# A two-layer graph network on one core: second-layer scores and weights moved behind other products, and adds of the output unit given to GpSimd

## The chip, the core and the metric

The kernel runs on one core of a Trainium2 chip. Its time is the device time of one execution in microseconds; the median of three runs is 2927.16 us (2926.97 to 2927.3). Engines are named TensorE (PE in the profile; its weight loads PEld), VectorE (DVE), ScalarE (ACT), GpSimd (POOL) and SyncE (SP, which issues the DMAs). Each engine works through its own instructions in the order in which the program gives them, and waits where an instruction needs what another engine has not finished.

## What is computed

64 graphs of 256 nodes with 512 features share one adjacency matrix; all is float32. Layer 0 is multi-head attention over neighbours, layer 1 a graph attention with one head, both with a layer norm and a ReLU ahead and a residual add behind:

```python
h = jnp.maximum(_layernorm(x, axis=-1), 0.0)
q, k, v = (h @ Wq + bq, h @ Wk + bk, h @ Wv + bv)        # 8 heads of 64
attn = softmax(q k^T / 8 + (1 - adj) * -1e9)
x = x + (attn v) @ Wo + bo
h = jnp.maximum(_layernorm(x, axis=-1), 0.0)
h = einsum('bnc,cf->bnf', h, W); s1, s2 = h @ a1, h @ a2
e = leaky_relu(s1[:, :, None] + s2[:, None, :], 0.2) * mask
x = x + elu(softmax(e, axis=2) @ h + beta * h)
```

## The kernel before, in words

**Pairs and products.** Graphs are worked on in pairs (32 of them, p = 0 to 31; graphs 2p and 2p+1). A product of a pair with a weight matrix is cut into 2 x 2 blocks (graphs by halves of the features), and seven block products take the place of eight (the Winograd form of Strassen's scheme). A `Unit` (L270) makes them: `p(i)` issues product i on TensorE. Products 1, 4, 5, 6 and 7 start a new PSUM bank (1 into `a`, 4 into `d`, 5 into `b`, 6 and 7 into `k`); product 2 adds into `a`, product 3 into `b`. With product 1 ScalarE copies `a` to `u2` (L283), with 6 VectorE adds `k` to `u2` (L285), with 7 it makes `u3` (L288). `products` (L640) calls `put11` after product 2, `put2` after 5 and `put12` after 3; these take the four blocks out of PSUM. Since product 3 adds into the bank of product 5, `put2` must have read that bank before. There are two QK units (queries and keys, L348), a V unit (L393), an O unit (L474) and a W unit (L579) for each pair. A QK product is 4 + 4 matmuls in the trace, the others 8.

**Layer 0.** `scores(b)` (L413): queries by keys (L422) into eight banks, the exponential on ScalarE (L426), the mask product and a pair sum on GpSimd (L427, L429). `values(b)` (L444): the weighted values (L440) and the row sums (L449) on TensorE; on VectorE a reciprocal (L451), the sums added to a running total `acc` for the range check (L452), the product (L454), and the reciprocal added to `acc` too (L455). `residual` (L468) loads the residual input y by DMA and adds the bias on GpSimd (L472); `o_blocks` (L458) forms two block sums on GpSimd (L464). The O unit's results are added to y: one VectorE operation for block (0,0) (L482), two for each of the other three (L486 and L487, or L492 and L493).

**Layer 1.** Statistics of y (L248), scales (VectorE L255, GpSimd L258 to L260, ScalarE L266), normalised h on ScalarE (L509). `node_sums` (L512) multiplies h by the projected attention vectors and sums, two operations for each tile of 128 nodes (L515). `gat_scores` (L518): two TensorE transposes spread the sums (the tile `pe`, L171), then on VectorE L525 twice and L527. `gat_exp` (L529): exponentials on ScalarE. `gat_divide` (L534): the weights, with beta on their diagonal (L539 twice). `gat_t` (L542): TensorE transposes them (the tile `at`, L548), ScalarE copies them (L549). `z_graph` (L551): h by weights (the tile `pz`, L561). Then the W unit and the ELU (L586 to L602), whose result goes out by DMA.

**Order.** It is written out by hand, the same for all engines: `start` (L719), `first` (L778), then for each pair `first_half` (L807) and `second_half` (L842), and `last` (L887) and `end` (L934) for the last pairs. The first half of pair p holds the V unit of pair p with the second layer's scores and weights of pair p-2 among its products (`v_chain`, L873), z and the W unit of pair p-2, and the O unit of pair p-1. The second half holds the rest of that O unit, the values of graph 2p, the scores of 2p+1, the QK units of pair p+1 with norms, node sums and `gat_scores` of graph 2p-1 among their products, and the values and scores that follow. At the start the weights' block sums (L120 to L123) and the projections of the attention vectors (L227) are put among the first pairs' work, and `in_range` (L701) checks at the end that no sum left the safe range; a general path runs only if one did.

Of the kernel before, what the change touches and what calls it, by code (L numbers as in the profile page):

```python
# [23 lines left out]
def kernel(ctx: ExitStack, tc: tile.TileContext, x, adj, wq, bq, wk, bk, wv, bv, wo, bo, w, a, beta, out):  # L24
# [65 lines left out]
    acc = const.tile([P, N], F32, name="acc")  # L90
    nc.gpsimd.memset(acc, 0.0)
# [9 lines left out]
    def weight(name, src, permuted=False):  # L101

        raw = const.tile([P, 3, 2, N], F32, name=f"{name}_b")
        b12 = blk("set", f"{name}_b12")
        tt = const.tile([P, 4, 2, N], F32, name=f"{name}_t")

        def fetch(*which):
            for j in which:
                dst, r, f = ((raw[:, 0], 0, 0), (raw[:, 1], 1, 0), (b12, 0, 1), (raw[:, 2], 1, 1))[j]
                if permuted:  # L110
                    for i in range(4):
                        nc.sync.dma_start(dst[i * HH:(i + 1) * HH], wo_rows(src)[r, i, :, :, f * N:(f + 1) * N])
                else:
                    nc.sync.dma_start(dst, rows_in_order(src)[r, :, :, f * N:(f + 1) * N])

        b11, b21, b22 = (raw[:, i] for i in range(3))
        t1, t2, t3, t4 = (tt[:, i] for i in range(4))

        def sums():
            nc.vector.tensor_tensor(t1, b12, b11, ALU.subtract)  # L120
            nc.vector.tensor_tensor(t2, b22, t1, ALU.subtract)
            nc.vector.tensor_tensor(t3, b12, b22, ALU.subtract)
            nc.vector.tensor_tensor(t4, b21, t2, ALU.subtract)  # L123

        return {1: b11, 2: b21, 3: b22, 4: t4, 5: t1, 6: t2, 7: t3}, b12, fetch, sums
# [47 lines left out]
    def project_b():  # L173


        WO, b12, fetch, sums = weight("wo", wo, True)
        fetch(*range(4))
        nc.sync.dma_start(bo2, bo.partition_broadcast(P))
        bvc = sb([P, DC], "bvc", "bvc", 1)
        with nc.allow_non_contiguous_dma(reason="a bias, once"):  # L180
            bv_v = bv.rearrange("(q i s d) -> i d q s", q=2, i=4, s=2, d=HH)
            for i in range(4):
                for q in range(2):
                    nc.sync.dma_start(bvc[i * HH:(i + 1) * HH, 2 * q:2 * q + 2], bv_v[i, :, q, :])
        cbs = []

        def part(n):
            if n == 0:
                sums()
            elif n == 1:  # L190
                for c in range(DC):
                    if c % 2 == 0:
                        cbs.append(sb([P, 2, P], "rec", f"bvb_{c}"))
                    nc.vector.tensor_scalar(cbs[-1][:, c % 2, :], ones, bvc[:, c:c + 1], None, ALU.mult)
            else:
                ps = bank("pbo")
                for c in range(DC):
                    for f in range(2):
                        b = ((WO[1], b12), (WO[2], WO[3]))[c // 2][f]
                        nc.tensor.matmul(ps[:, f * N:(f + 1) * N], cbs[c // 2][:, c % 2, :], b[:, c % 2, :],  # L200
                                         start=(c == 0 and f == 0), stop=(c == DC - 1), skip_group_check=True)
                nc.vector.scalar_tensor_tensor(bo2, bo2, -1.0, ps, op0=ALU.add, op1=ALU.add)

        return WO, part

    def project_a():
# [3 lines left out]
        sums()  # L210
# [28 lines left out]
        return part  # L239
# [62 lines left out]
    def combine_2(s):  # L302
        s[6] = blk(s["tag"], f"s2_{s['name']}")
        nc.vector.tensor_tensor(s[6], s[5], s[1], ALU.subtract)

    def combine_4(s):
        s[3] = blk(s["tag"], f"s4_{s['name']}")
        nc.vector.tensor_tensor(s[3], s[2], s[6], ALU.subtract)
# [135 lines left out]
    def values(b):  # L444
        for q in range(2):
# [6 lines left out]
            nc.vector.tensor_tensor(acc, sums[:, :N], acc, ALU.add)  # L452
            OT[b, q] = blk("set", f"oT_{b}_{q}")
            nc.vector.tensor_tensor(OT[b, q], two(ps), rec.unsqueeze(1).to_broadcast([P, 2, N]), ALU.mult)  # L454
            nc.vector.tensor_tensor(acc, acc, rec, ALU.add)  # L455
# [18 lines left out]
    class UnitO(Unit):  # L474

        def __init__(self, p):
            self.pair = p
            super().__init__(f"o_{p}", nodes_mm(A["o", p], WO))

        def put11(self):  # L480
            y = Y[2 * self.pair, 0]
            nc.vector.tensor_tensor(y, two(self.a), y, ALU.add)  # L482

        def put(self, gi, fh, ps, u):
            y = Y[2 * self.pair + gi, fh]
            nc.vector.tensor_tensor(two(ps), two(ps), u, ALU.add)  # L486
            nc.vector.tensor_tensor(y, two(ps), y, ALU.add)  # L487

        def put2(self):

            y = Y[2 * self.pair + 1, 1]
            nc.vector.tensor_tensor(two(self.k), two(self.b), self.u3, ALU.add)  # L492
            nc.vector.tensor_tensor(y, two(self.k), y, ALU.add)  # L493
            self.put(1, 0, self.d, self.u3)

        def put12(self):
            self.put(0, 1, self.b, self.u2)
# [81 lines left out]
    class UnitW(Unit):  # L579

        def __init__(self, p, tag=None):

            self.pair, self.o, self.tag = p, {}, tag
            super().__init__(f"w_{p}", nodes_mm(A.pop(("z", p)), WW))

        def elu(self, gi, fh, src, o=None, step=None):  # L586
# [7 lines left out]
            if step is not False:  # L594
                o, m, y = self.o[gi, fh]
                nc.vector.scalar_tensor_tensor(o, src, 0.0, y, op0=ALU.max, op1=ALU.add)  # L596
# [14 lines left out]
        def put2_sums(self):  # L611
            self.c = blk(self.tag or "c", f"o_{2 * self.pair + 1}_1")
            nc.vector.tensor_tensor(self.c, two(self.b), self.u3, ALU.add)
            nc.vector.tensor_tensor(two(self.d), two(self.d), self.u3, ALU.add)

        def put2_elu(self, step=None):

            self.elu(1, 1, self.c, self.c, step)
            self.elu(1, 0, two(self.d), None, step)

        def put12(self):
            nc.vector.tensor_tensor(two(self.b), two(self.b), self.u2, ALU.add)
            self.elu(0, 1, two(self.b))
# [65 lines left out]

    def residuals(p, which, tag="y"):  # L690
        for gi, fh in which:
# [9 lines left out]
    def in_range():  # L701
        bad = sb([P, 3], "bad", "bad", 1)
        for j, (src, op, bound) in enumerate(((acc, ALU.is_le, SAFE), (gsums, ALU.is_le, SAFE),
# [15 lines left out]
    def start():  # L719
# [24 lines left out]
        wo_blocks, shift = project_b()  # L744
# [19 lines left out]
        prods = project_a()  # L764
        products(uv, 4, 6)
        shift(1)
# [4 lines left out]
        shift(2)  # L771
# [4 lines left out]
        return wo_blocks, prods  # L776

    def first(prods):  # L778
# [4 lines left out]
        products(ua, 1, 4, 6, 2, 7, 5)  # L783
# [3 lines left out]
        products(ub, 4, 6, 7, 5, 2, 3)  # L787
        prods(3)
        prods(4)
# [5 lines left out]
        products(uv, 1, 4, 6, 2, 7, 5)  # L795
# [46 lines left out]
    def second_half(p, uo):  # L842
# [19 lines left out]
        ub.p(4)  # L862
        gat_scores(g1 - 2)
        gat_exp(g1 - 2)
        ub.p(6)
        y_sums(p - 1, 0, 0)
        products(ub, 7, 5)
# [5 lines left out]
    def v_chain(p):  # L873
# [7 lines left out]
        products(uv, 6, 2)  # L881
        gat_t(2 * p - 3)
        gat_t(2 * p - 4)
        products(uv, 7, 5)
        return uv

    def last():  # L887
# [6 lines left out]
        residuals(p - 1, ((0, 0), (1, 1), (1, 0), (0, 1)), "qk")  # L894
# [4 lines left out]
        uo = UnitO(p - 1)  # L899
# [4 lines left out]
        uw = UnitW(p - 2, "set")  # L904
# [4 lines left out]
        products(uw, 4)  # L909
        values(g1)  # L910
        y_normal(p - 1, 1)
        y_normal(p - 1, 0)
        residuals(p, ((0, 0), (1, 1)), "qk")
        o_blocks(p)
        residuals(p, ((1, 0), (0, 1)), "qk")
        products(uw, 6)
        y_sums(p - 1, 1, 0, 1)
        products(uw, 2, 7)
        uw.finish(0, 0, nc.gpsimd)
        gat_scores(g1 - 2)  # L920
        gat_exp(g1 - 2)
        uw.p(5)
        uw.put2_sums()
        uo = UnitO(p)
        uo.p(1)
        y_sums(p - 1, 0, 0)
        uw.put2_elu(False)
        uw.p(3)
        combine_24(A["o", p])
        y_sums(p - 1, 0, 1)  # L930
        uo.p(4)
        return uw, uo

    def end(uw, uo):  # L934
        p = NP - 1
        g0, g1 = 2 * p, 2 * p + 1
        products(uo, 2)
        uo.p(6)
        gat_scores(g0 - 2)
        gat_exp(g0 - 2)  # L940
        uw.put2_elu(True)
        uw.put12()
        uw.finish(1, 1, nc.gpsimd)
        uw.finish(1, 0, nc.gpsimd)
        uw.finish(0, 1, nc.gpsimd)
        products(uo, 7)
        divide(p - 1)
        products(uo, 5)
        y_stats(g1, NT, 0, g1, 1)
        y_stats(g1, NT, 0, g1, 0)  # L950
        rstd, mr = scales(f"y{g1}", 2)
        gat_t(g1 - 2)
        gat_t(g0 - 2)
        normal(g1, rstd, minus(mr, f"y{g1}"), "v")
        y_stats(g0, NT, 0, g0, 0)
        products(uo, 3)
        y_stats(g0, NT, 0, g0, 1)
        rstd, mr = scales(f"y{g0}", 2)
        z_graph(p - 1, 0)
        z_graph(p - 1, 1)  # L960
        normal(g0, rstd, minus(mr, f"y{g0}"), "v")
        y_sums(p, 1, 0, 1)
        gat_scores(g1)
        z_31(p - 1)
        gat_exp(g1)
        z = A["z", p - 1]
        combine_2(z)
        uw = UnitW(p - 1, "pt")
        products(uw, 1, 4)
        y_sums(p, 0, 0, 1)  # L970
        products(uw, 6)
        gat_divide(ATT[g1], gsums[:, NT * g1:NT * g1 + NT], g1)
        uw.p(2)
        gat_scores(g0)
        gat_exp(g0)
        uw.p(7)
        gat_t(g1)
        uw.put11()
        uw.p(5)
        uw.put2_sums()  # L980
        combine_4(z)
        uw.finish(0, 0, nc.gpsimd)
        z_graph(p, 1)
        gat_divide(ATT[g0], gsums[:, NT * g0:NT * g0 + NT], g0)
        uw.p(3)
        gat_t(g0)
        uw.put2_elu()
        uw.put12()
        uw.finish(1, 1, nc.gpsimd)
        uw.finish(1, 0, nc.gpsimd)  # L990
        uw.finish(0, 1, nc.gpsimd)
        bad = in_range()
# [4 lines left out]
        combine_24(A["z", p])  # L997
        uw = UnitW(p, "pt")
        uw.p(1)
        uw.p(4)  # L1000
        uw.p(6)
        uw.p(7)
# [12 lines left out]
    with tc.manual_schedule(engines={ENG.PE, ENG.DVE, ENG.Activation, ENG.Pool}):  # L1015
        WW = {}
        WO, prods = start()
        second_half(1, first(prods))
# [166 lines left out]
```

## Time and profile before

| | |
|---|---|
| median of 3 runs | 2927.16 us |
| profiled execution: its time, its span | 2926.01 us, 2924.1 us |
| granted TensorE clock, mean | 0.998 |
| instructions | 46443 |
| VectorE: L515, 256 times | 253.7 us, mean 1.04 us |
| VectorE: L451, 128 times | 224.3 us, mean 1.75 us |
| VectorE: L452 and L455, 128 times each | 46.4 and 92.5 us |
| GpSimd: L427, 512 times | 710.8 us, mean 1.39 us |
| DMA | 110 MB, 38 GB/s over the span |

The span is from the first to the last instruction of the profiled execution. In lists of instructions each line has the start in us from the beginning of the span, the duration, engine, line of the program, operation, the tiles (written <- read), the shapes and the count; a bracket at the end gives the idle time of the engine before it and what ended that.

### The profile page before, as it was taken

To read this page: it belongs to the slowest core of one execution; us is meant where nothing else is said; L and a number is where in the kernel's file an instruction comes from. 1 tells how busy PE (TensorE), PEld (TensorE's weight loads), DVE (VectorE), ACT (ScalarE), POOL (GpSimd) and SP (SyncE) were. 2 spreads that over 40 slices of the span, in tenths; PEclk is the share of its full clock that TensorE was granted. 3 is DMA by queue.
4 is the path that set the end of the run, shared out by engine and by line. 5 is a ranking of instruction groups with operands and counts; after the bars stand their busy time and mean duration, and the time that the engine had idled before them with its cause. 6 is when DMAs were issued, how large, how long until landed. Compare 5 with 4: busy or idle time off the path is not lost.

```text
span 2924.1 us, 46443 instructions
## 1 busy us (share of the span) xinstructions
PE 2815.4 (96%) x18110; PEld 2344.7 (80%) x18110; DVE 2158.2 (74%) x3779; ACT 1035.7 (35%) x2116; POOL 1525.4 (52%) x1464
## 2 busy tenths in 40 slices
PE   9999999999999999999999999999999999999998
PEld 7887788787888878888778887788787888878876
DVE  7677877777777677776787777877777777678776
ACT  3233334333333333333343333334333333333323
POOL 4645545455454554545554545545455454555572
PEclk9999999999999999999999999999999999999999
DMA  5010011100111100111001110011100111100101
GB/s 148 5 44 17 28 44 44 44 23 29 37 44 44 33 26 30 44 44 44 15 30 44 44 44 20 26 44 44 44 27 26 37 44 44 33 26 30 37 30 44
DMA packets 96479, 110.00 MB, mean 38 GB/s; under 512 B 8576, under 2 KB 79488, under 8 KB 96256
## 3 DMA queue, kind: packets, MB, share of 16 engines
q1 hardware_dynamic: 96256, 106.99, 11.7%
q8 instruction: 145, 2.38, 0.3%
q14 instruction: 78, 0.64, 0.1%
HBM read 73.41 MB, written 33.55 MB: 37 GB/s over the span
## 4 chain that ended last, share of the span: by engine, by line


## 5 line engine op out<-in xcount | busy, mean ns | idle before, releaser
L427 POOL TENSOR_TENSOR pt<-pt,maskT 128x512 f32<-128x512 f32 x512 | 710.8, 1388 | 799.9 <-ACT pt L426 799.9
L429 POOL TENSOR_TENSOR pp<-pt 128x256 f32<-128x256 f32 x512 | 429.1, 838 | 40.1
L426 ACT ACTIVATE pt<-sc 128x512 f32<-128x512 f32 x512 | 257.7, 624 | 411.2 <-PE sc L422 411.2
L451 DVE RECIPROCAL rec<-sm 128x256 f32<-128x256 f32 x128 | 224.3, 1753 | 46.5 <-PE sm L449 46.5
L515 DVE SCALAR_TENSOR_TENSOR pr<-h,war 128x512 f32<-128x512 f32 x256 | 253.7, 1035 | 0.0
L440 PE MATMUL av<-pt,v 128*32 128x256 f32 x4096 | 246.0, 381 | 0.7 <-DVE v L410 0.7
L422 PE MATMUL sc<-qk 64*128 64x256 f32 x2048 | 238.4, 382 | 0.0
L422 PEld LDWEIGHTS sc<-qk 64*128 64x128 f32 x2048 | 192.8, 187 | 46.1 <-issue 13.1
L561 PE MATMUL pz<-eT,h 128*128 128x256 f32 x1024 | 226.5, 379 | 0.7 <-ACT eT L549 0.7
L601 POOL TENSOR_TENSOR o<-o,m 128x512 f32<-128x512 f32 x29 | 36.9, 1272 | 346.7 <-ACT m L591 334.7
L561 PEld LDWEIGHTS pz<-eT,h 128*128 128x128 f32 x1024 | 194.5, 190 | 27.3 <-ACT eT L549 0.9
L440 PEld LDWEIGHTS av<-pt,v 128*32 128x32 f32 x4096 | 126.6, 110 | 99.0 <-issue 21.7
L564 ACT COPY z<-pz 128x512 f32<-128x512 f32 x128 | 74.9, 587 | 244.2 <-PE pz L561 244.1
L472 POOL TENSOR_TENSOR y<-y,bo 128x512 f32<-128x512 f32 x128 | 161.3, 1283 | 0.0
L374 DVE SCALAR_TENSOR_TENSOR qk<-qk_p,bq,qk_u 128x256 f32<-128x256 f32 x192 | 92.1, 480 | 80.1 <-PE qk_p L356 80.0
L532 ACT ACTIVATE e<-e 128x256 f32<-128x256 f32 x128 | 52.2, 409 | 250.6 <-DVE e L527 250.6
L539 DVE SCALAR_TENSOR_TENSOR e<-e,grec,betai 128x256 f32<-128x256 f32 x128 | 134.2, 1087 | 2.3
L356 PE MATMUL qk_p<-h,wq_b 128*128 128x256 f32 x512 | 134.7, 386 | 0.3 <-ACT h L333 0.2
L596 DVE SCALAR_TENSOR_TENSOR o<-w_p,y 128x512 f32<-128x512 f32 x87 | 60.2, 692 | 99.7 <-ACT m L590 99.7
L509 ACT ACTIVATE h<-y,nmr_y,rstd_y 128x256 f32<-128x256 f32 x256 | 132.5, 591 | 1.1
L356 PE MATMUL qk_p<-h,wk_t 128*128 128x256 f32 x512 | 131.5, 379 | 0.0
L356 PE MATMUL qk_p<-s_h,wq_t 128*128 128x256 f32 x512 | 131.5, 379 | 0.0
(177 smaller groups left out, 6209.0 us busy)
## 6 DMA issues: line engine op xcount, KB each, us to landing
x<-in_x_dram SPq DMA_DIRECT2D x128, 256.0 KB, 2.8
y<-in_x_dram SPq DMA_DIRECT2D x128, 256.0 KB, 2.8
out_dram<-o SPq DMA_DIRECT2D x116, 256.0 KB, 2.5
out_dram<-y SPq DMA_DIRECT2D x11, 256.0 KB, 2.1
wq_b<-in_L_gnn_Wq_dram SPq DMA_DIRECT2D x4, 256.0 KB, 6.0
wk_b<-in_L_gnn_Wk_dram SPq DMA_DIRECT2D x4, 256.0 KB, 6.3
wv_b<-in_L_gnn_Wv_dram SPq DMA_DIRECT2D x4, 256.0 KB, 4.9
wo_b<-in_L_gnn_Wo_dram SPq DMA_DIRECT2D x16, 64.0 KB, 3.1
```

The lines of the kernel that those rows point to most:

```text
L356: nc.tensor.matmul(ps[:, j * N:(j + 1) * N], wj[i][:, c, ft * P:(ft + 1) * P], s[i][:, c, :], start=(start and j == 0 and c == 0), stop=(c ...
L422: nc.tensor.matmul(pss[2 * pair + h][:, k * N:(k + 1) * N], qk[hs, 1, k * P:(k + 1) * P], qk[hs, 0, :], start=True, stop=True)
L426: nc.scalar.activation(pt, two(pss[i]), AF.Exp, scale=QSCALE)
L427: nc.gpsimd.tensor_tensor(pt, pt, maskT, ALU.mult)
L429: nc.gpsimd.tensor_tensor(pp, pt[:, 0, :], pt[:, 1, :], ALU.add)
L440: nc.tensor.matmul(ps[i * HH:(i + 1) * HH, s * N:(s + 1) * N], v[:, k, c0:c0 + HH], pts[i][:, k, :], start=(k == 0), stop=(k == NT - 1))
L451: nc.vector.reciprocal(rec, sums[:, :N])
L472: nc.gpsimd.tensor_tensor(r, r, bo2[:, fh * N:(fh + 1) * N].unsqueeze(1).to_broadcast([P, 2, N]), ALU.add)
L509: nc.scalar.activation(h2[t][:, f * N:(f + 1) * N], Y[g, f][:, t, :], AF.Relu, bias=nmr[:, t:t + 1], scale=rstd[:, t:t + 1])
L515: nc.vector.scalar_tensor_tensor(pr, H2[g][t], 1.0, war[:, j, :], op0=ALU.mult, op1=ALU.mult, accum_out=SC[g][:, t, j:j + 1])
L539: nc.vector.scalar_tensor_tensor(e[:, t, :], e[:, t, :], rec[:, t:t + 1], betai[:, (1 - t) * P:(3 - t) * P], op0=ALU.mult, op1=ALU.add)
L561: nc.tensor.matmul(ps[:, f * N:(f + 1) * N], h2[k][:, fs], eT[:, k, :], start=(k == 0), stop=(k == NT - 1))
```

## The change

Five things are done; most of the diff is the order of the last pairs.

1. In the second half, `gat_scores` and `gat_exp` of graph 2p-1 move from behind product 4 of the second QK unit to behind its product 7. In `v_chain` both `gat_t` move from ahead of product 7 of the V unit to behind it.
2. The O unit adds u2 or u3 to y ahead of time on GpSimd (three adds, after products 6 and 7), and one VectorE operation then adds the PSUM bank to y. Only unit p = 30 has its adds on VectorE.
3. In `values`, L452 and L455 become one VectorE operation that adds sums and reciprocal in PSUM and puts the row total in a column of `checks`; `in_range` looks at that.
4. The block sums of Wo and W, and the projections, are spread over `first` instead of `start`.
5. `last` and `end` have a new order; W units 29 and 30 (`pooled`) do part of the ELU on ScalarE and GpSimd.

```diff
@@ values
-            nc.vector.tensor_tensor(acc, sums[:, :N], acc, ALU.add)
+            i = 2 * b + q
+            nc.vector.scalar_tensor_tensor(sums[:, :N], sums[:, :N], 1.0, rec, op0=ALU.mult, op1=ALU.add,
+                                           accum_out=checks[:, i:i + 1])
             OT[b, q] = blk("set", f"oT_{b}_{q}")
             nc.vector.tensor_tensor(OT[b, q], two(ps), rec.unsqueeze(1).to_broadcast([P, 2, N]), ALU.mult)
-            nc.vector.tensor_tensor(acc, acc, rec, ALU.add)
@@ UnitO
+        def p(self, i):
+            super().p(i)
+            if i == 6:
+                self.ahead(0, 1, self.u2)
+            if i == 7:
+                self.ahead(1, 1, self.u3)
+                self.ahead(1, 0, self.u3)
+
+        def ahead(self, gi, fh, u):
+            y = Y[2 * self.pair + gi, fh]
+            self.eng.tensor_tensor(y, y, u, ALU.add)
+
+        def put(self, gi, fh, ps):
+            y = Y[2 * self.pair + gi, fh]
+            nc.vector.tensor_tensor(y, two(ps), y, ALU.add)
...
         def put2(self):
-
-            y = Y[2 * self.pair + 1, 1]
-            nc.vector.tensor_tensor(two(self.k), two(self.b), self.u3, ALU.add)
-            nc.vector.tensor_tensor(y, two(self.k), y, ALU.add)
-            self.put(1, 0, self.d, self.u3)
+            self.put(1, 1, self.b)
+            self.put(1, 0, self.d)
@@ UnitW.elu
-                nc.vector.scalar_tensor_tensor(o, src, 0.0, y, op0=ALU.max, op1=ALU.add)
+                if self.pooled and (gi, fh) != (0, 0):
+                    nc.scalar.activation(src, src, AF.Relu)
+                    nc.gpsimd.tensor_tensor(o, src, y, ALU.add)
+                else:
+                    nc.vector.scalar_tensor_tensor(o, src, 0.0, y, op0=ALU.max, op1=ALU.add)
@@ first
-        products(ua, 1, 4, 6, 2, 7, 5)
+        wo_sums(0, 1)
+        products(ua, 1, 4, 6)
+        wo_sums(2, 3)
+        products(ua, 2, 7, 5)
         prods(2)
         ub.p(1)
         products(ua, 3)
-        products(ub, 4, 6, 7, 5, 2, 3)
-        prods(3)
-        prods(4)
+        products(ub, 4, 6)
+        w_sums(0, 1)
+        products(ub, 7, 5)
+        w_sums(2, 3)
+        products(ub, 2, 3)
...
-        products(uv, 1, 4, 6, 2, 7, 5)
+        products(uv, 1, 4, 6)
+        prods(3)
+        products(uv, 2, 7, 5)
+        prods(4)
@@ second_half
         ub.p(4)
+        ub.p(6)
+        ub.p(7)
         gat_scores(g1 - 2)
         gat_exp(g1 - 2)
-        ub.p(6)
         y_sums(p - 1, 0, 0)
-        products(ub, 7, 5)
+        products(ub, 5)
@@ v_chain
-        products(uv, 6, 2)
+        products(uv, 6, 2, 7)
         gat_t(2 * p - 3)
         gat_t(2 * p - 4)
-        products(uv, 7, 5)
+        products(uv, 5)
@@ last
-        uo = UnitO(p - 1)
+        uo = UnitO(p - 1, nc.vector)
...
+        uw.p(7)
+        y_sums(p - 1, 1, 0)
+        products(uw, 2)
+        y_sums(p - 1, 1, 1)
         uw.finish(0, 0, nc.gpsimd)
+        uo = UnitO(p)
+        products(uo, 1, 2)
+        combine_2(A["o", p])
+        uo.p(4)
         gat_scores(g1 - 2)
         gat_exp(g1 - 2)
@@ end
+        y_sums(p - 1, 0, 0)
+        uo.p(7)
+        divide_1(g1 - 2)
+        y_sums(p - 1, 0, 1)
+        uo.p(5)
+        uo.put(1, 1, uo.b)
+        uw.p(5)
+        gat_t(g1 - 2)
         gat_scores(g0 - 2)
         gat_exp(g0 - 2)
...
```

## The prediction, on record before the changed kernel ran

> **What bounds the kernel now.** I read the page first, then who waits for whom on TensorE, then the order in time of one pair (90.25 us from pair to pair, alike from pair 2 to pair 30), engine by engine, and last the stretch from 2800 us to the end.
>
> The page's first part (busy time by engine):
>
> ```profile
> PE 2815.4 (96%) x18110; PEld 2344.7 (80%) x18110; DVE 2158.2 (74%) x3779; ACT 1035.7 (35%) x2116; POOL 1525.4 (52%) x1464
> ```
>
> TensorE sets the time; what is to be won is its idle time. The waits of TensorE alone (total us, times, longest):
>
> ```profile
> PE pe L171 <- DVE pr L515: 59.6, 32, 2.6
> PE at L548 <- DVE e L539: 31.8, 31, 3.6
> PE v_p L389 <- DVE v L406: 2.4, 1, 2.4
> ```
>
> Two waits, once in each pair, are nearly all of it: the transposes of the second layer's scores (pe), and of its weights (at). In one pair (start, us, instruction):
>
> ```profile
> 1414.93 0.27 PE L171 MATMUL pe<-ident,s 128*128 128x128 f32 x1
> 1417.08 0.32 PE L171 MATMUL pe<-ident,s 128*128 128x128 f32 x1 [1.87 <-DVE pr L515]
> ...
> 1441.30 0.71 PE L548 MATMUL at<-ident,e 128*128 128x128 f32 x5
> 1442.95 0.55 PE L548 MATMUL at<-ident,e 128*128 128x128 f32 x3 [0.93 <-DVE e L539]
> ...
> 1477.87 1.91 PE L331 MATMUL tr<-ident,x 128*128 128x128 f32 x16
> 1479.61 1.89 PE L389 MATMUL o_p<-wo_b,s_o 128*128 128x256 f32 x8
> ```
>
> Transposes else start 0.11 apart, so the first wait loses 1417.08 - 1414.93 - 0.11 = 2.04 us, and the second 1442.95 - 1441.30 - 5 x 0.11 = 1.10. The last line, the output unit's product 3, waits for nothing now; it matters below. VectorE at the same two places:
>
> ```profile
> 1412.46 1.75 DVE L515 SCALAR_TENSOR_TENSOR pr<-h,war 128x512 f32<-128x512 f32 x1
> ...
> 1417.73 0.86 DVE L525 SCALAR_TENSOR_TENSOR e<-pe,s,adj_sb 128x256 f32<-128x256 f32 x2
> 1418.63 0.75 DVE L527 SCALAR_TENSOR_TENSOR e<-e 128x512 f32<-128x512 f32 x1
> ...
> 1477.80 0.68 DVE L288 TENSOR_TENSOR o_u<-o_p,o_u 128x512 f32<-128x512 f32 x1
> 1478.58 0.70 DVE L492 TENSOR_TENSOR o_p<-o_p,o_u 128x512 f32<-128x512 f32 x1
> ```
>
> The sums before pe (L515) take up to 1.75 where others of the same line take 0.68: GpSimd runs its mask products meanwhile. GpSimd around the output unit:
>
> ```profile
> 1471.83 2.50 POOL L472 TENSOR_TENSOR y<-y,bo 128x512 f32<-128x512 f32 x2
> 1487.73 1.27 POOL L427 TENSOR_TENSOR pt<-pt,maskT 128x512 f32<-128x512 f32 x1 [13.40 <-ACT pt L426]
> ```
>
> It is idle from 1474.3 to 1487.7, which is where the three new adds fall. Times to be used: a product is 1.73 on TensorE (eight matmuls, 0.216 apart); VectorE sees a product 0.20 after its end (L288 at 1408.23, product ended 1408.03), TensorE starts 0.06 after VectorE's end (1417.02 to 1417.08), GpSimd 0.10 after (mv_y, 1406.23 to 1406.33).
>
> **Scores two products later.** TensorE passes products 6 and 7 of the second QK unit first, 3.45 us against a wait of 2.04, so that wait goes: 29 x 2.03 and 1.49 in pair 1 = 60.4 us. On VectorE L525 twice and L527 (0.90 + 0.61) now stand behind the sum of product 7 (L288), and queued behind them are the two L515 of y_sums(0,0) and the four L374 of product 5. Product 3 of that unit adds into the bank that the first two L374 read, so TensorE waits for those. From the end of product 7: 0.20, L288 0.60, L525s 0.90, L527 0.61, two L515 1.22, two L374 0.87, 0.06 = 4.46 us. TensorE has in that time two transposes 0.27, product 5 and product 2 (3.45) = 3.72. **A new wait of 0.74 us**, times 30 = +22.2. That the wait is for both L374, not one, I take from the trace: L374 for a first half starts at 1409.96, after the whole product (1409.75), though its half was done 0.86 earlier; banks are waited for whole. Bounds: 0.35 if the half sufficed, 1.2 if GpSimd's mask products still run beside L527 and the L515s (they end at 1419.97 now, before that point).
>
> **Weights one product later.** TensorE passes product 7 (1.73) before at, against a wait of 1.10. The weights are ready at 1442.80, 6.5 us after L525 began, and that chain starts from pe as before. So 30 x 1.10 = -33.0. Next late would be the ScalarE copy of at (0.59 each, two), with product 5's 1.73 ahead of its reader: the last copy ends some 0.9 after the last transpose, cover enough; without it up to 1.0 a pair.
>
> **The adds on GpSimd.** VectorE loses three of seven operations of an output unit (0.69 each), GpSimd gets three adds of two SBUF tiles, 1.27 each by L601 and L472. VectorE's time is worth nothing by itself; the order is. Before: L288 ended 1478.48, L492 read the bank at 1478.58 to 1479.28, product 3 began at 1479.61 with 0.27 in hand. Now: L285 ends 1476.68, the first add starts behind L601 on VectorE (two SBUF inputs, to 1477.28) and is done about 1478.5; L288 ends 1478.48; the add for block (1,1) runs 1478.58 to 1479.85; VectorE's put (1,1), the only reader of the bank, 1479.90 to 1480.59; product 3 at 1480.65. **A second new wait of 1.04 us**, 29 times (pair 1's unit has no backlog on VectorE) = +30.2. Behind the waiting put stand put (1,0), two L248, two L339, put (0,1) and the reciprocal of the next sums; they reach it at about 1484.3, before the delayed sums are there (1484.9), so nothing more is lost. The cost lies between 0 (put before 1479.55) and 2.3 (the put waits for the third add too); I take the sum.
>
> Here a rule speaks against the change. The row: L515 is 0.68 alone and 1.75 beside a mask product, while L285, L288 and L374, with one input in PSUM, keep 0.69 and 0.48 beside them. The Trainium skill, "SBUF — State Buffer", section "SBUF: two separate sides", says that GpSimd and a VectorE operation of two SBUF inputs hold a shared port pair for a whole instruction, and the other blocks. By the rule alone 3 x 1.27 = 3.8 us of lock a pair could stop VectorE, 110 us in all. By the rows only L601 stands in that window with two SBUF inputs, and it is there first; the lock costs 0.4 on the first add, which ends before it is needed. I go by the rows.
>
> **One range check operation.** L452 (0.36) and L455 (0.72) become one operation with one PSUM input and an accumulator; nearest rows L374 (0.48) and L227 (0.42 with its 0.08 readout). 128 times about -0.6 = 77 us of VectorE, none of it waited for by TensorE. Bounds: 0.40 to 0.55 between its neighbours. v_p starts at 1434.07, 0.09 after the chain's end (1433.98), so 0.55 would cost up to 0.3 a pair, 9 us; a shorter one gains nothing. I take 0. The memset and the final check: 0.
>
> **Start.** The weight sums leave the first 57 us: the wait for L406 (2.55 with the restart) and one of 1.02 go. Product sums (L227) now follow put2 of V unit 1, so the pwa transposes (111.19 now) wait until about 112.8: +1.6. Net -2; between -4 and +2.
>
> **Last pair.** After 2840 us the rows show 15.9 us lost: pe 2.75 and 2.08, at 3.81 and 1.0, 2.9 around the last z, and slow matmuls behind the long waits:
>
> ```profile
> 2867.65 2.20 PE L548 MATMUL at<-ident,e 128*128 128x128 f32 x8 [3.65 <-DVE e L539]
> 2869.64 3.04 PE L389 MATMUL o_p<-wo_b,s_o 128*128 128x256 f32 x8
> ```
>
> The new order puts three products (5.2) more ahead of pe and spreads the divides. Against it: unit 30's adds stay on VectorE, two of them beside mask products, so its product 3 waits about 1.4; the sums for the last W pair wait for statistics, some 5 in all by my count. The finishing adds moved behind W's combines carry their output DMAs on SP with them, and the last pair's four residual loads are issued together (2.8 us to landing); both are waited for by no product here. Net -7, between -13 and +2.
>
> **The sum.** -60.4 - 33.0 + 22.2 + 30.2 - 2 - 7 = -50. Per pair 90.25 - 2.03 - 1.10 + 0.74 + 1.04 = 88.90. The profiled execution took 2926.01 (span 2924.1 and 1.9 around it), so 2876; the runs' median lies 1.15 above it: 2877.
>
> **Rivals.** (1) Both new waits, as summed: 2877, its own range 2862 to 2893; chance 0.55. (2) One of them is hidden, because the adds or L374 come earlier than I reckon: 2847 or 2855; 0.17. (3) Neither comes: -102, 2825; 0.05. For it: TensorE has no other idle time; against: the two chains above are lengths of rows. (4) The gain is smaller: the old waits are replaced by longer ones (GpSimd beside L527: +0.5; put (1,1) late by another 0.5), or the pe wait only moves along: 2893 to 2918; 0.15. (5) Slower: the handover from VectorE to GpSimd and back holds product 3. It decides from a wait of 1.04 + 50/29 = 2.8 us. If the put stood behind all three adds after L288 (3.8 + 0.8, minus 1.1 in hand) it would be 3.5: +71, 2948. For it: L288 is 1.45 late already; against: GpSimd is idle for 13.4 us there, and the first add needs only L285. 0.08, of which 0.02 near the balance.
>
> What can be told from no change is 0.2%, 5.9 us. Faster 0.92, same 0.02, slower 0.06. The range 2845 to 2908 leaves out case 3, half of 4's upper part and 5, under 2 in 10.
>
> **What would show it.** In the profile after: pe and at gone from TensorE's waits; qk_p L356 waiting for L374 about 0.7, and o_p L389 for the put on VectorE about 1.0, 30 times each; VectorE's put waiting for GpSimd's y 1.3 us; pairs 88.9 apart; GpSimd busy up by 3.8 a pair; VectorE down by some 140. Wrong if o_p waits for nothing (then near 2847), if the at or eT wait stays, or if the puts wait for three adds.

## The result and the profile after

The changed kernel takes 2898.55 us (median of 4 runs, 2898.09 to 2899.54), the kernel before 2927.09 beside it (2926.97 to 2927.3). The ratio is 0.9903, 95% interval 0.9886 to 0.992: faster by 28.5 us, 1.0%. The forecast was 2877; the time lies inside its range, and the gain is little more than half of the 50 us that the sum gave. The profiled span went from 2924.1 to 2896.3 us.

Lines move by a few in the changed program: pe L171 is L169, at L548 is L551, the node sums L515 are L518, L525 and L527 are L528 and L530, the QK unit's output L374 is L369, L285 and L288 are L280 and L283, L454 is L451. New are the GpSimd adds (L486), the one VectorE operation that puts a block into y (L490) and the range check operation (L448).

Busy time by engine, from the page after:

```profile
PE 2818.8 (97%) x18110; PEld 2344.3 (81%) x18110; DVE 2035.7 (70%) x3678; ACT 1041.7 (36%) x2122; POOL 1647.2 (57%) x1564
```

VectorE lost 122 us and GpSimd gained 122, and neither number is the gain. TensorE's waits after (us in total, times, longest):

```profile
PE o_p L384 <- DVE y L490: 25.7, 31, 1.1
PE qk_p L351 <- DVE qk L369: 22.7, 31, 0.8
PE pwa L169 <- DVE wa L225: 3.1, 1, 3.1
...
PE at L551 <- DVE e L542: 1.9, 3, 1.0
...
PE pe L169 <- DVE pr L518: 1.5, 2, 0.9
```

The two old waits, 59.6 and 31.8 us, are gone from the pairs. Two new ones stand in their place, at the two instructions and behind the two lines that the prediction named. The third, at pwa near the start, is new too; 1.6 us was forecast there. One pair on TensorE after:

```profile
1287.69 1.91 PE L326 MATMUL tr<-ident,x 128*128 128x128 f32 x16
1290.44 1.99 PE L384 MATMUL o_p<-wo_b,s_o 128*128 128x256 f32 x8 [0.84 <-DVE y L490]
...
1319.57 0.38 PE L169 MATMUL pe<-ident,s 128*128 128x128 f32 x2
...
1322.38 1.03 PE L351 MATMUL qk_p<-h,wk_b 128*128 128x256 f32 x4
1324.17 1.13 PE L351 MATMUL qk_p<-s_h,wq_b 128*128 128x256 f32 x4 [0.76 <-DVE qk L369]
...
1343.16 1.04 PE L551 MATMUL at<-ident,e 128*128 128x128 f32 x8
```

Here pe and at run in one piece. A bracket is not all that a wait costs. Four matmuls start 0.86 after those before them where nothing waits; from 1322.38 to 1324.17 it is 1.79, so 0.93 is lost and not 0.76. The four that waited last 1.13, not 1.03: another 0.10. The output unit's product 3 starts 2.75 after the transposes ahead of it (1287.69 to 1290.44), where it was 1.74 before (1477.87 to 1479.61): 1.01 lost at a bracket of 0.84, and 0.10 again (1.99 for 1.89). VectorE at these two places:

```profile
1287.63 0.68 DVE L283 TENSOR_TENSOR o_u<-o_p,o_u 128x512 f32<-128x512 f32 x1
1289.69 0.69 DVE L490 TENSOR_TENSOR y<-o_p,y 128x512 f32<-128x512 f32 x1 [1.39 <-POOL y L486]
1290.92 0.69 DVE L490 TENSOR_TENSOR y<-o_p,y 128x512 f32<-128x512 f32 x1 [0.54 <-POOL y L486]
...
1319.13 0.67 DVE L280 TENSOR_TENSOR qk_u<-qk_p,qk_u 128x512 f32<-128x512 f32 x1
1319.90 0.69 DVE L283 TENSOR_TENSOR qk_u<-qk_p,qk_u 128x512 f32<-128x512 f32 x1
1320.51 0.86 DVE L528 SCALAR_TENSOR_TENSOR e<-pe,s,adj_sb 128x256 f32<-128x256 f32 x2
...
1323.64 0.47 DVE L369 SCALAR_TENSOR_TENSOR qk<-qk_p,bk,qk_u 128x256 f32<-128x256 f32 x1
```

u3 (L283) is done at 1288.31, GpSimd adds it to y, and only then, 1.39 us later, can the put read the bank (1289.69 to 1290.38) that TensorE's product 3 (1290.44) adds into. In the other place TensorE starts product 3 at 1324.17, 0.06 after the second L369 (1324.11): it does wait for both. GpSimd at the first place:

```profile
1286.65 4.24 POOL L486 TENSOR_TENSOR y<-y,o_u 128x512 f32<-128x512 f32 x3 [2.49 <-DVE o_u L280]
```

**Where the 27.8 us of span come from.** On TensorE's own times: the start, up to the values that follow the O unit in the second half of pair 1, is 5.4 us longer; 29 pairs from there are 2585.0 us instead of 2616.9, so 31.9 shorter (1.10 a pair); the rest of pair 30 is 2.2 shorter; the last pair 0.9 longer.

### The profile page after: what moved, and what is told of

The parts are those of the page before. It is cut to its first block, busy times and chain, and to the rows that moved or that the text cites. A ratio compares the mean times of both kernels' runs of the same rounds, so it can differ in the third digit from the quotient of the medians.

```text
span 2896.3 us, 46339 instructions
## 1 busy us (share of the span) xinstructions
PE 2818.8 (97%) x18110; PEld 2344.3 (81%) x18110; DVE 2035.7 (70%) x3678; ACT 1041.7 (36%) x2122; POOL 1647.2 (57%) x1564
## 4 chain that ended last, share of the span: by engine, by line
## 5 line engine op out<-in xcount | busy, mean ns | idle before, releaser
L424 POOL TENSOR_TENSOR pp<-pt 128x256 f32<-128x256 f32 x512 | 417.1, 815 | 40.1
L518 DVE SCALAR_TENSOR_TENSOR pr<-h,war 128x512 f32<-128x512 f32 x256 | 265.4, 1080 | 0.0
L486 POOL TENSOR_TENSOR y<-y,o_u 128x512 f32<-128x512 f32 x93 | 126.7, 1377 | 90.1 <-DVE o_u L280 82.6
L351 PE MATMUL qk_p<-h,wq_t 128*128 128x256 f32 x512 | 131.5, 379 | 0.0
```

What stands on the lines that cost most here:

```text
L351: nc.tensor.matmul(ps[:, j * N:(j + 1) * N], wj[i][:, c, ft * P:(ft + 1) * P], s[i][:, c, :], start=(start and j == 0 and c == 0), stop=(c ...
L424: nc.gpsimd.tensor_tensor(pp, pt[:, 0, :], pt[:, 1, :], ALU.add)
L518: nc.vector.scalar_tensor_tensor(pr, H2[g][t], 1.0, war[:, j, :], op0=ALU.mult, op1=ALU.mult, accum_out=SC[g][:, t, j:j + 1])
```

## Experiments

Periods below are the median distance in TensorE's time from one pair's at transposes to the next: 90.25 before, 89.13 after. What a place loses in a pair is taken from start to start, as above, and so is more than its bracket. Kernels named "before plus" are the kernel before with one thing added; the others start from the kernel after. The kernel before took 2926.2 to 2926.4 beside all of them.

**1. Part 1 alone (p_moves).** Before plus the moves of scores and weights:

```diff
         ub.p(4)
+        ub.p(6)
+        ub.p(7)
         gat_scores(g1 - 2)
         gat_exp(g1 - 2)
-        ub.p(6)
         y_sums(p - 1, 0, 0)
-        products(ub, 7, 5)
+        products(ub, 5)
...
-        products(uv, 6, 2)
+        products(uv, 6, 2, 7)
         gat_t(2 * p - 3)
         gat_t(2 * p - 4)
-        products(uv, 7, 5)
+        products(uv, 5)
```

> Before with part 1 alone: scores two products later, weights one later, nothing else. My theory: both old waits of TensorE go (2.03 and 1.10 us a pair), and the wait of product 3 of the second QK unit for the two L374 comes with the move itself, 0.8 to 1.2 us a pair, because the order on VectorE makes it and the adds on GpSimd have no part in it: 2855 to 2872 us. Rival: that wait comes only with the adds and their effect on the sums before it; then all 3.1 us a pair are won, about 2832 us.

Measured: 2858.03 us, ratio 0.9769 (0.9753 to 0.9786), 40 us faster than the whole change; period 87.91. Its waits on TensorE:

```profile
PE qk_p L356 <- DVE qk L374: 18.9, 30, 0.6
PE pe L171 <- DVE pr L515: 4.3, 2, 2.6
PE at L548 <- DVE e L539: 3.6, 1, 3.6
```

What is left of pe and at lies in the last pairs. The first new wait belongs to this part, and its sum (-60.4 - 33.0 + 22.2 = -71) is right to 3 us.

**2. Part 2 alone (p_ahead).** Before plus the three adds on GpSimd and the single puts, the UnitO of the diff shown with the change; its core:

```diff
+            if i == 6:
+                self.ahead(0, 1, self.u2)
+            if i == 7:
+                self.ahead(1, 1, self.u3)
+                self.ahead(1, 0, self.u3)
```

> Before with part 2 alone: the output unit's adds on GpSimd, in all units (the last pairs keep their old order). My theory: product 3 of the output unit waits 0.9 to 1.0 us for the put that now stands behind a GpSimd add, 29 times or more: 2927 + 27 to 32 = 2954 to 2960 us. Rival (the adds relieve VectorE, which then reaches the sums for pe sooner): 2927 us or less.

Measured: 2954.34 us, ratio 1.0094 (1.0077 to 1.0111): slower by 28. Its waits:

```profile
PE pe L171 <- DVE pr L522: 43.6, 32, 1.9
PE at L555 <- DVE e L546: 33.6, 33, 4.1
PE o_p L389 <- DVE y L494: 30.4, 30, 6.2
```

The third line is the price of the handover. The pe wait fell from 59.6 to 43.6 at the same time: the four node sums ahead of it met GpSimd's operations otherwise and took 4.95 us in place of 5.47, and pe lost 1.49 in place of 2.03 (experiments 3, 8 and 9 are about this). So the period grew by 0.56 only (16 us over 29 pairs), and the rest is in the last pairs, where one put waits so long that product 3 loses 6.2.

**3. Part 3 alone (p_check).** Before plus the one operation for the range check:

```diff
-            nc.vector.tensor_tensor(acc, sums[:, :N], acc, ALU.add)
+            nc.vector.scalar_tensor_tensor(sums[:, :N], sums[:, :N], 1.0, rec, op0=ALU.mult, op1=ALU.add,
+                                           accum_out=checks[:, i:i + 1])
...
-            nc.vector.tensor_tensor(acc, acc, rec, ALU.add)
```

> Before with part 3 alone: one range check operation for two. My theory: VectorE loses some 75 us of work, none of which TensorE waits for: 2927 us, within 4. Rival: the sums for pe start sooner or meet fewer mask products on GpSimd, the pe wait shrinks by 0.3 us a pair or more: 2918 us or less.

Measured: 2900.17 us, ratio 0.9913 (0.9896 to 0.9929). My theory, that shorter work which nobody waits for is worth nothing, fell. The loss at pe is 1.20 us a pair, not 2.03, and the wait ahead of at has a bracket of 0.74, not 0.93. The node sums ahead of pe, on VectorE in this kernel:

```profile
1400.47 0.71 DVE L515 SCALAR_TENSOR_TENSOR pr<-h,war 128x512 f32<-128x512 f32 x1
...
1401.11 1.20 DVE L515 SCALAR_TENSOR_TENSOR pr<-h,war 128x512 f32<-128x512 f32 x1
...
1402.25 1.74 DVE L515 SCALAR_TENSOR_TENSOR pr<-h,war 128x512 f32<-128x512 f32 x1
...
1403.92 1.20 DVE L515 SCALAR_TENSOR_TENSOR pr<-h,war 128x512 f32<-128x512 f32 x1
```

In the kernel before the four are 0.99, 1.75, 1.20, 1.74 in the pair shown in the prediction. They run beside GpSimd's mask products and pair sums. From the first one's start to the last one's end (they overlap a little) the four took 5.47 us before and 4.65 here, medians over the pairs: 0.82 less, the same as the 0.83 by which the loss at pe fell. The 0.6 us of an operation don't account for that. My reading was that it matters where in GpSimd's run the sums begin; experiments 8 and 9 test it.

**4. Part 4 alone (p_start).** Before plus the block sums and projections spread over `first`, as in the diff shown with the change; its core:

```diff
-        products(ub, 4, 6, 7, 5, 2, 3)
-        prods(3)
-        prods(4)
+        products(ub, 4, 6)
+        w_sums(0, 1)
+        products(ub, 7, 5)
+        w_sums(2, 3)
+        products(ub, 2, 3)
```

> Before with part 4 alone: the weight sums and projections spread over the first pairs. My theory: pwa waits about 3 us for product sums that meet GpSimd's mask products, TensorE is slow for some matmuls behind it, the memset of betai on GpSimd stands behind those mask products too and holds an output product about 1 us; the wait at 55 us stays: 2927 + 4 to 6 = 2931 to 2933 us. Rival (the loss at the start seen in the changed kernel comes from the other parts): 2925 us.

Measured: 2932.89 us, ratio 1.0022 (1.0013 to 1.0031): 6.6 slower, all of it at the start. In its waits there is one that the kernel before lacks:

```profile
PE pwa L170 <- DVE wa L226: 3.3, 1, 3.3
```

**5. The first new wait taken out of the whole (a_ysum).** After, with the two node sums that stand ahead of L369 put behind it, into the call that made the next two anyway:

```diff
-        y_sums(p - 1, 0, 0)
         products(ub, 5)
-        y_sums(p - 1, 0, 1)
+        y_sums(p - 1, 0, 0, 1)
```

> The changed kernel with one pair of node sums (two L518 of graph 2p-2) moved behind the put of product 5 of the second QK unit, so that the two L369 that read the bank come 1.22 us sooner. My theory: the bank's reader on VectorE holds product 3; its wait (0.93 us and 0.10 of restart, 30 times) goes: 2898.5 - 31 = 2866 to 2871 us. Rival: another instruction ends that wait soon after (the pe tile, ScalarE's copies, GpSimd), or the sums that come later delay the next pe: 2885 us or more.

Measured: 2867.59 us, ratio to before 0.9802 (0.9785 to 0.9818); qk_p is gone from the waits, o_p keeps its 25.6; period 88.12. So this wait costs 89.13 - 88.12 = 1.01 a pair and 31 us in all.

**6. The second one taken out (a_no11).** After, with block (1,1) added the old way, on VectorE, in all but the last two pairs:

```diff
-                self.ahead(1, 1, self.u3)
+                if self.pair >= NP - 2:
+                    self.ahead(1, 1, self.u3)
...
-            self.put(1, 1, self.b)
+            if self.pair >= NP - 2:
+                self.put(1, 1, self.b)
+            else:
+                nc.vector.tensor_tensor(two(self.k), two(self.b), self.u3, ALU.add)
+                self.put(1, 1, self.k)
```

> The changed kernel with block (1,1) of the output unit put as before in all pairs but the last two (VectorE adds bank and u3 in PSUM, then y), so that no GpSimd add stands ahead of the reader of product 5's bank; two adds stay on GpSimd. My theory: the wait of product 3 of the output unit (0.89 and 0.10 of restart, 29 times) goes: 2898.5 - 29 = 2867 to 2873 us. Rival: GpSimd's load beside VectorE costs it, the put of (1,0) or the reciprocal behind it becomes late, and less than half is won: 2885 us or more.

Measured: 2867.06 us, ratio 0.9798 (0.9781 to 0.9814); o_p is gone, qk_p keeps its 22.6; period 88.03. This wait costs 1.10 a pair and 31 us. One of the three adds, given back to VectorE, is enough.

**7. What is good of the change without what costs (n_best1).** Before plus parts 1 and 3, with the node sums moved as in a_ysum; no adds on GpSimd, start and end as before. The second half then reads:

```diff
         ub.p(4)
+        ub.p(6)
+        ub.p(7)
         gat_scores(g1 - 2)
         gat_exp(g1 - 2)
-        ub.p(6)
-        y_sums(p - 1, 0, 0)
-        products(ub, 7, 5)
-        y_sums(p - 1, 0, 1)
+        products(ub, 5)
+        y_sums(p - 1, 0, 0, 1)
```

> Before with parts 1 and 3 (later scores and weights, one range check operation), and the same pair of node sums behind the put of product 5; no adds on GpSimd, start and last pairs as before. My theory: no wait of TensorE is left in a pair: 2926.3 - 30 x 3.13 = 2832, with restarts 2830 to 2838 us. Rival (VectorE or GpSimd then bounds a pair): 2845 us or more, with a wait at v_p, at or the scores.

Measured: 2832.25 us, ratio 0.9679 (0.9663 to 0.9695). The page's line by engine:

```profile
PE 2806.0 (99%) x18110; PEld 2348.0 (83%) x18110; DVE 2062.8 (73%) x3779; ACT 1040.6 (37%) x2116; POOL 1508.9 (53%) x1463
```

The period is 87.12, and both old waits are gone. That it is 90.25 - 2.03 - 1.10 to the hundredth is chance. By TensorE's times the two places gave back 2.08 and 1.15, restarts included, and 0.10 came in elsewhere: the QK product behind the scores starts 0.05 after VectorE's range check operation ends (1442.81 to 1442.86); in the kernel before nothing is lost there. GpSimd is less busy than before, and TensorE has 99% of its span.

**8. Less work for VectorE in another place (p_no455).** Before, without L455, so that the reciprocals are left out of the range check. It shortens the same stretch as part 3 and was to tell whether less work or its place did it.

```diff
-            nc.vector.tensor_tensor(acc, acc, rec, ALU.add)
```

> Before without L455, the add of the reciprocal to the running total (this leaves the reciprocals out of the range check); L452 stays. Theory after part 3 alone won 26 us: L455 has two SBUF inputs and stands between the sums and the statistics while GpSimd runs its mask products; without it those products come sooner against the node sums, which then meet shorter ones. So L455 alone gives most of it: 2898 to 2908 us. Rival: it is the total of VectorE work ahead of the sums, L452 as much as L455; then 2910 us or more.

Measured: 2963.91 us, ratio 1.0128 (1.0111 to 1.0145): one VectorE operation less makes the kernel 37 us slower. The theory, 2898 to 2908, missed: less work for VectorE is not what wins. The four sums take 5.64 us, pe loses 2.19 (2.03 in the bracket), and then, on TensorE:

```profile
1435.40 0.32 PE L171 MATMUL pe<-ident,s 128*128 128x128 f32 x1 [2.03 <-DVE pr L514]
1435.56 1.35 PE L356 MATMUL qk_p<-s_h,wq_t 128*128 128x256 f32 x4
1436.70 1.91 PE L356 MATMUL qk_p<-s_h,wk_t 128*128 128x256 f32 x4
1438.41 1.59 PE L356 MATMUL qk_p<-s_h,wq_t 128*128 128x256 f32 x4
1439.83 1.03 PE L356 MATMUL qk_p<-s_h,wk_t 128*128 128x256 f32 x4
```

Four matmuls take up to 1.91 instead of 1.03: some eight of them start 0.43 apart, not 0.216. The table of stretches of the same kernel (length, then busy time of TensorE, its loads, VectorE, ScalarE, GpSimd, and then the granted clock) has it as a clock:

```profile
1433.00:1436.00 3.00, 0.97 (x7) 0.57 (x6) 3.00 (x6) 0.00 (x0) 2.84 (x3) 1.00 0.00 0
1436.00:1439.50 3.50, 3.50 (x10) 2.79 (x9) 2.38 (x6) 0.91 (x4) 0.00 (x0) 0.52 0.00 0
1439.50:1443.00 3.50, 3.50 (x17) 3.09 (x17) 2.20 (x6) 0.00 (x0) 0.00 (x0) 0.99 0.00 0
```

The clock is halved for 3.4 us after the gap, which costs 8 x 0.21 = 1.7 us. With 0.16 more lost at pe and 0.2 less at the at transposes that makes +1.67 a pair, the period measured (91.92). The gain of part 3 would be the same coupling with the other sign, shorter sums in place of longer ones; experiment 9 tests that.

**9. Part 3 with GpSimd moved instead (p_check_delay).** p_check, with five small memsets on GpSimd behind the statistics' scales, ahead of the mask products; VectorE's work is that of p_check.

```diff
+        for _ in range(5):
+            nc.gpsimd.memset(idle, 0.0)
...
-        scores(g1, {(0, 2): lambda: y_scales(p - 1)})
+        scores(g1, {(0, 2): lambda: (y_scales(p - 1), pause())})
```

> The kernel with part 3 alone (2900 us), and five small memsets on GpSimd behind the scales of each pair, some 0.8 us, so that the mask products that follow stand later against the node sums; VectorE has the same work. Theory now: what part 3 won is the phase of the two engines on their shared lock, since the four sums took 4.7 us there and 5.5 or 5.6 before and without L455. The delay brings back the long phase, the pe wait grows by 0.8 us or more a pair: 2920 to 2930 us, and up to 2965 us if the wait passes 2.1 us and TensorE is slow behind it as without L455. Rival: VectorE's own work decides: 2894 to 2906 us.

Measured: 2958.63 us, ratio 1.0095 (1.0064 to 1.0125). With VectorE's operations as in p_check, some 58 us are lost by delaying GpSimd. The four sums are 5.69 us, pe loses 2.24, and in 23 of the 28 pairs from 200 to 2800 us a stretch of slow matmuls follows (in p_no455 in 22 of 28). Its four runs go from 2945.8 to 2969.4 us, and their mean granted clock from 0.990 to 0.984; which pairs are hit is told in the last section. VectorE's operations are those of p_check and only the time at which GpSimd's begin differs, so this run shows that it is the phase of the two engines that part 3 changes.

| kernel | four sums ahead of pe, first start to last end, us | loss at pe, us | slow matmuls behind | period |
|---|---|---|---|---|
| p_check | 4.65 | 1.20 | 0 | 89.33 |
| p_ahead | 4.95 | 1.49 | 0 | 90.81 |
| before | 5.47 | 2.03 | 0 | 90.25 |
| p_no455 | 5.64 | 2.19 | 8 in most pairs | 91.92 |
| p_check_delay | 5.69 | 2.24 | 8 in most pairs | 92.04 |
| after | 5.68 | 0 | 0 | 89.13 |

In every row but the last the loss is the four sums less 3.45 us, so what TensorE waits for there is these sums and nothing else. The last row says why part 3's gain is not in the whole: the sums are as slow as in the worst kernel, and with pe behind products 6 and 7 nobody waits for them.

**10. The end as before (a_oldend).** After, with the last pairs in the old order, and with the adds of the last two output units on VectorE as before:

```diff
-        uo = UnitO(p - 1, nc.vector)
+        uo = UnitO(p - 1)
...
-        uw = UnitW(p - 2, "pt", True)
+        uw = UnitW(p - 2, "set")
```

> The changed kernel with the last pairs as before (last, end, the W units' ELU, and the output units of the last two pairs). My theory: the new order of the last pairs is worth nothing: 2896 to 2900 us. Rival: it wins the 7 us that were forecast, and something else at the end costs them: 2904 us or more.

Measured: 2896.8 us (2894.7 to 2899.2), ratio 0.9896 (0.9879 to 0.9912), beside 0.9903 (0.9886 to 0.992) for the whole change. The new order of the end, most of the diff, is worth nothing that these runs can tell.

**11. A better start (n_best3).** n_best1 with the block sums spread as in the change, but the output shift (pbo) ahead of the product sums, and product sums 3 and 4 where they were.

```diff
             if n == 0:
-                sums()
-            elif n == 1:
...
         shift(1)
         products(uv, 2)
         prods(0)
...
-        shift(2)
...
-        products(ua, 1, 4, 6, 2, 7, 5)
+        wo_sums(0, 1)
+        products(ua, 1, 4, 6)
+        wo_sums(2, 3)
+        products(ua, 2, 7, 5)
```

`shift(1)` is the output shift here, and was the step ahead of it.

> The best so far (2832 us: parts 1 and 3, node sums behind the put of product 5) with the weight sums spread as in part 4, but the bias product pbo ahead of the product sums that need its buffers, and product sums 3 and 4 where they were before. My theory: the wait at 55 us (2.4 us, not the weight sums' doing, since VectorE waits there for pbo to give its buffers back) and the 0.7 us behind it go, and pwa does not wait: 2827 to 2830 us. Rival: the weight sums among the first pairs hold a product there: 2832 us or more.

Measured: 2829.9 us (2828.47 to 2830.41), ratio 0.967 (0.9654 to 0.9686), 2.4 below n_best1. The wait of v_p for L406, 2.4 in all kernels above, is gone. It is the fastest kernel of this study: 96 us below before.

**12. Two adds on GpSimd and the new end on top (n_best2).** n_best1 with the adds for blocks (0,1) and (1,0), as in a_no11, and with the new end. Of the adds:

```diff
+            if i == 6:
+                self.ahead(0, 1, self.u2)
+            if i == 7:
+                if self.pair >= NP - 2:
+                    self.ahead(1, 1, self.u3)
+                self.ahead(1, 0, self.u3)
```

> The best so far (2832 us) with two of the three adds of each output unit on GpSimd (not that of block (1,1)) and the new order of the last pairs; start as before. My theory: VectorE's relief is worth nothing where TensorE waits for nothing, and the last pairs are worth nothing: 2830 to 2836 us. Rival: the adds on GpSimd cost or win 0.2 us a pair through the lock: under 2827 or over 2839 us.

Measured: 2830.75 us, ratio 0.9672 (0.9656 to 0.9688), period 87.02. Against n_best1 the two harmless adds and the new end together give 1.5 us. The 0.10 that the period is shorter is the new loss behind the scores, which is gone here. So this period is the one with nothing but the two old waits taken out: 90.25 - 2.08 - 1.15 = 87.02.

## Why the prediction was right in its mechanism and 22 us off

| term | predicted, us | measured | by |
|---|---|---|---|
| pe and at waits go | -3.13 a pair | -3.23 | TensorE's times; n_best2 against before |
| new wait for L374 (X) | +0.74 a pair | +0.90 alone, +1.01 in the whole | TensorE's times in p_moves; after against a_ysum |
| new wait for the put (Y) | +1.04 a pair | +1.10 | after against a_no11 |
| range check operation | 0 | -26 alone; no sign of it in the whole | p_check; the sum of the lines above |
| start | -2 | +5.4 (+6.6 alone) | TensorE's times; p_start |
| last pair | -7 | +0.9 | TensorE's times; a_oldend |

**The two old waits, right to 0.10.** The forecast left out the restarts behind them, 0.05 each. And nothing further was late behind them: nobody waits for the copies of at, named as next, in the pairs.

**X, the right place and too small.** The sum set 4.46 us of VectorE's chain against 3.72 of TensorE's work. The chain is right: in the pair shown it takes from the end of product 7 (1319.73) to 1324.17, 4.44. TensorE's side is not: pe starts at 1319.57, and product 3 could start at 1319.57 + 0.22 + 3.45 = 1323.24, only 3.51 after that end, because the end in a row of matmuls lies 0.16 behind the start of the next. So the wait is 0.93, and 0.10 of restart comes on top; the sum left out the restart, and its 3.72 is 0.21 too long. In p_moves, where L288 starts 0.20 behind the start of pe and not 0.33, the wait is 0.13 less. In the whole L280 ends at 1319.80 and L283 follows with 0.10 between them: VectorE arrives later there, as its four sums are longer (5.68 against 5.47).

**Y, right.** The put waits 1.39 for the add (1.3 was forecast), and product 3 loses 1.01 and 0.10 where 1.04 was forecast. That VectorE's lock on the shared port would not stop the output unit was right too: L283 and the puts keep 0.68 and 0.69 beside GpSimd's 4.24 us of adds. The third add makes the second put wait 0.54, which nobody waits for.

**The check operation, right in the whole by luck.** "None of it waited for by TensorE" is wrong as a step: alone, this edit is worth 26 us. The sums it moves end in pe, which TensorE did wait for, and they meet GpSimd's mask products in a different phase. In the whole the pe wait is gone by other means. No run took part 3 out of the whole, but the sum leaves nothing for it: -3.23 + 1.01 + 1.10 = -1.12, and the period went from 90.25 to 89.13. This is also, for the most part, why the parts don't add up: -68, +28, -26, +6.6 and about 0 make -60, and the whole is -28. Parts 1 and 3 are paid out of the same wait.

**The start, the step that failed first.** I took the weight sums to be what made v_p wait for L406. They were not. The product sums stand ahead of it on VectorE, and after the change still do, released at 51.37 by TensorE's pbo, which gives back a buffer that they use. VectorE in the kernel after:

```profile
51.37 1.25 DVE L222 SCALAR_TENSOR_TENSOR prod<-w_b,a 128x256 f32<-128x256 f32 x1 [6.14 <-PE pbo L196]
...
120.22 0.29 DVE L227 TENSOR_SCALAR betai<-ident,beta 128x128 f32<-128x128 f32 x1 [6.10 <-POOL betai L226]
```

n_best3, with pbo ahead of the product sums, loses that wait; p_start, with the weight sums gone from there, does not. The second line is a cost that I did not look for: betai is cleared by a memset of 0.42 us on GpSimd, which now stands behind GpSimd's mask products, and VectorE waits 6.10 for it. On TensorE the delay arrives twice:

```profile
114.27 1.94 PE L169 MATMUL pwa<-ident,wa 128*128 128x128 f32 x8 [3.09 <-DVE wa L225]
116.00 2.73 PE L384 MATMUL o_p<-wo_b,oT 128*128 128x256 f32 x8
...
123.05 1.97 PE L384 MATMUL o_p<-wo_t,s_o 128*128 128x256 f32 x8 [0.86 <-DVE s_o L299]
```

pwa waits 3.09 where 1.6 was forecast, since product sums 3 take up to 1.47 us beside GpSimd's mask products and 0.42 elsewhere; pwa (1.94 for 1.04) and the product behind it (2.73 for 1.89) then run slowly; and a later product waits 0.86 for sums queued behind betai.

**The last pair.** I had counted 15.9 us of old losses and some 5 of new ones. After the change the large waits are gone there too, and many small ones (pz, at, w_p, pe, o_p, each 0.3 to 1.8) with the restarts make about as much. My count of new waits was a guess where I had no chain of rows. a_oldend shows that the total is right to about 2 us; it does not tell the single waits apart, and that stays open.

**The rivals.** By its number the result lies in case 4, a smaller gain (2893 to 2918, chance 0.15), and outside the 2862 to 2893 that case 1 gave itself. By its mechanism it is case 1: both new waits came where they were named, and neither grew by the half microsecond of case 4 (X by 0.27, Y by 0.06). Of the 22 us short, 7.2 are the 29 pairs (1.10 each in place of 1.35), 7.4 the start and 7.9 the last pair. The slower case has its mechanism shown in p_ahead at a smaller size: the handover alone is +28, of which 12 lie in the last pairs.

## What to carry to other kernels

Moving an operation later on the engine that waits for it moves everything queued behind it on the engine that makes it. Look for what in that queue frees a buffer or a bank, as L369 did behind two node sums here, and let it pass first. An add handed to a third engine is free only where nobody needs its result soon; two of three were free here and the third cost 31 us. Try the parts of a change one by one: the best kernel here leaves out the adds on GpSimd and the new end, and moves something else in what it keeps.

## What the runs showed of the hardware beyond the forecast

- **Less work can be slower.** VectorE's operations with two SBUF inputs and GpSimd's take turns: the rule of the Trainium skill, "SBUF — State Buffer", section "SBUF: two separate sides", that whichever starts first holds the shared pair for its whole instruction, fits 0.71 or 1.20 or 1.74 for the same L515. It gives no phase. Here four such sums took 4.65 to 5.69 us by phase alone, and the kernel 2900 to 2959 us.
- **2.0 us of idle time in one window cost TensorE its clock.** In each run the slow stretches begin on one grid of 3.41 us. Cut along that grid, the traces of the 14 kernels have 10622 windows from 150 to 2740 us. After 45 of them the granted clock was 0.5 for the next window, and those 45 had 2.01 us or more without a matmul; none of the others reached 2.01. So the gap at pe in p_no455 (bracket 2.03) costs the clock where it lies inside one window, as in 22 of 28 pairs, and not where it runs across a boundary. The 1.87 of the kernel before never does. The wait of v_p for L406, 2.4 us near the start of 13 kernels, was followed by a slow stretch in 5. The Trainium skill, "TensorE: Matmul & The Clock Gate", section "What's actually happening", has an idle window of about 3.4 us ahead of the slow state; the length of the slow stretch agrees, but the idle time needed is shorter in these runs.
- **A wait costs about a quarter of a microsecond more than its bracket.** Brackets of 0.76 and 0.84 cost 1.01 and 1.10 a pair (a_ysum, a_no11). Of that, 0.16 is the end of the row ahead, which lies behind the start that the next row would have had, and 0.10 is lost at the second matmul after the wait (1.13 for 1.03, 1.99 for 1.89).
